# Layer 0's in-degrees from packed tiles: adds on GpSimd and one-column products instead of ones-products of every tile

## The chip, the cores and the metric

One core of a Trainium2 chip runs the kernel alone; seven cores are idle. The metric is device time in microseconds (us) of one execution. The engines are PE (TensorE, matrix products), PEld (its weight loads), DVE (VectorE), ACT (ScalarE), POOL (GpSimd) and SP (here only an issuer of DMAs). Each works through its own list of instructions in order; an instruction that waits for another engine holds up all that stand behind it on its own.

## What is computed

The input is a feature matrix `x` of 2708 x 512 and a 0/1 adjacency matrix `adj` of 2708 x 2708 in int32. Four graph layers follow each other, each on the layer-normed, rectified output of the one before, and each is added to its input. Only layer 0 is touched:

```python
h = relu(layernorm(x))
a = adj.astype(float32)
out = (a.T @ h) @ weight
in_degree = a.sum(axis=0)                    # column sums of adj
out = out * clip(in_degree, 1.0, None)[:, None] ** (-0.5)
x = x + relu(out)
```

Layers 1 to 3 need the transposed 0/1 pattern and the row sums of `adj`, and layer 0's pass over `adj` prepares both.

## The kernel before

The 2708 rows are cut into `NC` = 22 blocks of `R` = 128 rows (the last has 20). The 22 column blocks are cut into six **groups** g of 4, 4, 4, 4, 3 and 3 blocks (line 104). Layer 0 goes through 6 x 22 units (g, m): group g of columns against row block m. A group's results gather in PSUM, one bank of 128 x 512 for each of its `K` column blocks (`acc`, line 577); PSUM has 8 such tiles (`ps`, line 125), which are used in rotation.

`staged` (line 244) writes the program as a software pipeline: in step s it emits `load0` of unit s, `count0` of unit s-4, `sign0` of s-5 and `multiply0` of s-7 (lines 660 to 668). While group 0 runs, the layer norm of `x` and the products with the weight (`h_ps`, line 186) are made too, so PE has twice the work in that group.

- `load0` (487) fetches a 128 x 512 int32 tile `ai` of `adj` (10 buffers). Row blocks 0 to 19 are fetched in pairs, rows 2r of a pair in one tile and rows 2r+1 in the next.
- `count0` (518): ACT squares `ai` into the fp32r tile `ar` (523), which PE will use. DVE makes the running row sum `cum` in int16 (scan, 529) and copies its last column into `deg` (537). For every even m DVE packs two tiles into one int16 tile, `two` = 256 * next + this (541), three buffers. `two` has an int16 for each column, whose low byte is one row's 0 or 1 and whose high byte is the next row's.
- `sign0` (553): ACT turns `cum` into a sum of signs.
- `multiply0` (567): POOL starts the DMA that writes `two` to DRAM (574), from where layer 1 fetches it transposed. PE multiplies `ar` with the halves of `h0[m]` into `acc` (403), two matmuls for each column block, one for m = 21.

The **in-degrees** are column sums of `adj`, so they are sums over partitions, which PE makes: with each of the 22 tiles of a group, K products with a 128 x 32 tile of ones (`oneb`, 592). The tile is read as bf16, every second half-word, which is exact for 0 and 1. They come in batches after m = 3, 7, 11, 15 and 19 (lines 580 to 598; the last takes m = 16 to 21) and add up to 484 matmuls. The sums lie along the free dimension; at m = 19 ACT copies them to SBUF (`by_col`, 601), at m = 21 PE transposes them (607), and DVE, ACT and DVE make `nrm` = max(sum, 1) ** -0.5 of them (611, 618, 619). At the end of the group the K banks of `acc` are scaled by `nrm` and rectified, the even ones on ACT (645), the odd ones on DVE (640), into three buffers of the tag "t", and POOL adds `x` (648; DVE does it in the last group). The next group's fourth `acc` reuses the bank of the first of these.

`fenced` (509) sets a priority: `count0` and `sign0` of later units are put behind the named ACT and DVE instructions of the eviction, so that the tile scheduler doesn't emit them first. The scheduler decides the order on each engine when the program is built; it puts some `two` instructions ahead of scans.

After the last unit `deg` is written to DRAM and fetched back transposed as `rdeg` (685 to 692), and DVE waits for that (695) ahead of the layer norms of layer 1. Layer 1's first products (`nb_ps`, `line_ps`, line 186) begin while layer 0's last group runs.

Of the kernel before, what the change touches and what calls it, by code (L numbers as in the profile page):

```python
# [8 lines left out]
F32 = mybir.dt.float32  # L9
F32R = mybir.dt.float32r  # L10
BF16 = mybir.dt.bfloat16
I32 = mybir.dt.int32
I8 = mybir.dt.int8
I16 = mybir.dt.int16
AF = mybir.ActivationFunctionType
# [29 lines left out]
def fast_layers(  # L45
# [46 lines left out]
    def rows(c):  # L92
        return min(R, N - c * R)
# [358 lines left out]
    with ExitStack() as ring_ctx:  # L452
# [30 lines left out]
        with tc.tile_pool(name="l0", bufs=2) as wk:  # L483
            units = [(g, m) for g in range(len(groups)) for m in range(NC)]
            tiles, uppers, acc, sums, xs = {}, {}, {}, {}, {}
# [32 lines left out]
            def count0(i):  # L518
# [20 lines left out]
                if m % 2 == 0:  # L539
                    two = wk.tile([R, WG + P - R], I16, name="two", bufs=3)  # L540
                    nc.vector.scalar_tensor_tensor(
                        two[:, :wide],
                        tiles[i + 1][0][:, :wide],
                        256.0,
                        ai[:, :wide],
                        op0=ALU.mult,
                        op1=ALU.add,
                    )
                    if wide < KR + P - R:
                        nc.gpsimd.memset(two[:, wide : KR + P - R], 0)  # L550
                tiles[i] = ar, cum, two
# [15 lines left out]
            def multiply0(i):  # L567
# [11 lines left out]
                uppers[m] = ar.bitcast(BF16)  # L579
                batch = range(0)  # L580
                if m == NC - 3:
                    for j in (1, 2):
                        uppers[m + j] = tiles[i + j][0].bitcast(BF16)
                    batch = range(m // 4 * 4, NC)
                elif m % 4 == 3:
                    batch = range(m - 3, m + 1)
                if m == 3:
                    sums[g] = ps.tile([P, 2 * P], F32, name="sums_ps", tag="ps")
                for j in batch:
                    q = rows(j)  # L590
                    for k in range(K):
                        nc.tensor.matmul(
                            sums[g][k * 32 : (k + 1) * 32, :R],
                            oneb[:q],
                            uppers[j][:q, 2 * k * R + 1 : 2 * (k + 1) * R : 2],
                            start=(j == 0),
                            stop=(j == NC - 1),
                        )
                if m == NC - 3:
                    by_col = sums[g, 0] = common.tile([P, D], F32, name="by_col", tag="t", bufs=3)[:, :R]  # L600
                    ins = nc.scalar.copy(by_col[: K * 32], sums[g][: K * 32, :R])
                    fences["act"] = ins.ins
                for k, c in enumerate(cs):
                    matmuls(acc[c], h0[m], ar, k, m)
                if m == NC - 1:
                    pt = sums.pop(g)[:R, P:]
                    nc.tensor.transpose(
                        pt[:, : K * 32], sums.pop((g, 0))[: K * 32], ident[: K * 32, : K * 32]
                    )
                    nrm = sums[g, 1] = small.tile([R, KMAX, 1], F32, name="nrm")  # L610
                    nc.vector.tensor_scalar(
                        nrm[:, :K],
                        pt[:, : K * 32].rearrange("p (k j) -> p k j", j=32)[:, :, :1],
                        1.0,
                        None,
                        op0=ALU.max,
                    )
                    nc.scalar.activation(nrm[:, :K], nrm[:, :K], AF.Sqrt)
                    ins = nc.vector.reciprocal(nrm[:, :K], nrm[:, :K])
                    fences["dve"] = ins.ins  # L620
# [9 lines left out]
                nrm = sums.pop((g, 1))  # L630
# [1401 lines left out]
```

## Time and profile before

| | |
|---|---|
| three runs | 1802.83 us median, 1800.16 to 1804.46 |
| profiled execution | 1800.19 us, its span 1798.3 us |
| granted TensorE clock | 0.995 of full speed |
| PE busy | 1767.9 us (98% of the span) |
| DVE busy | 1309.7 us (73%) |
| ACT busy | 816.0 us (45%) |
| POOL busy | 248.7 us (14%) |
| `sums_ps` products, line 592 | 484 matmuls, 14.2 us busy |
| scans, line 529 | 132, mean 1.18 us with `deg` and 1.21 us without |

The span's first 36 us prepare fused weights for layer 3. Layer 0 takes the stretch from about 39 to 376 us: start and group 0 to 174 us, three groups of four column blocks of 43.2 us each, two groups of three to 376 us. Layer 1 then runs to about 760 us, and layers 2 and 3 take the rest. Busy times are unions of an engine's instructions; matmuls are pipelined, so a busy PE can still be waiting. What ended an idle stretch is inferred from semaphore events.

### The profile page before, as it was taken

The page shows a single profiled execution, that of the slowest core. Times are in us where ns is not written, and L with a number is a line of the kernel's source. Part 1 is how long each engine was busy: PE and PEld are TensorE (multiplying, and loading weights), DVE is VectorE, ACT ScalarE, POOL GpSimd, SP SyncE. Part 2 cuts the span into 40 slices and gives each one's busy share as a digit, 9 for nine tenths or more (in the row PEclk, how much of TensorE's full clock was granted, in tenths as well). Part 3 has the DMA queues.
Part 4 walks back from the last instruction along what each step waited for, and adds up shares of the span by engine and source line. Part 5 has one row for each costly group of instructions (what it writes and reads, how often), then busy time and mean ns, then how long its engine had stood idle before and what let it go on. Part 6 is the DMA issues. An engine that isn't in the chain of part 4 may idle for free.

```text
span 1798.3 us, 30708 instructions
## 1 busy us (share of the span) xinstructions
PE 1767.9 (98%) x11880; PEld 1050.8 (58%) x11880; DVE 1309.7 (73%) x1842; ACT 816.0 (45%) x1554; POOL 248.7 (14%) x245
## 2 busy tenths in 40 slices
PE   9899999999999999999999999999999999999998
PEld 4456777654448888644454444444444455588786
DVE  4952998855446655888999999999999777633334
ACT  2643777732210000156887767767774566400000
POOL 0101332311111211266000000000001222100000
PEclk9999999999999999999999999999999999999999
DMA  7632666634451211243220121121022444313221
GB/s 251 199 106 71 210 204 192 205 80 119 122 142 50 69 55 47 86 147 123 74 62 25 45 63 44 27 63 50 19 68 60 141 134 133 107 43 99 71 71 40
DMA packets 166445, 176.06 MB, mean 98 GB/s; under 512 B 83454, under 2 KB 105918, under 8 KB 165394
## 3 DMA queue, kind: packets, MB, share of 16 engines
q1 hardware_dynamic: 143738, 130.61, 25.7%
q10 hardware_dynamic: 18808, 33.37, 4.9%
q0 software_dynamic: 3744, 10.03, 1.5%
q8 instruction: 95, 1.56, 0.4%
q14 instruction: 60, 0.49, 0.1%
HBM read 110.60 MB, written 55.36 MB: 92 GB/s over the span
## 4 chain that ended last, share of the span: by engine, by line
PE 86%; DVE 7%; issue 3%; DMA 3%; ACT 1%; POOL 1%; DVEq 0%; SPq 0%; ACTq 0%; POOLq 0%
PE acc L403 33%; PE av L1110 19%; PE nb_ps L186 8%; PE sums L1110 6%; PE wh_ps L186 4%; PE self_ps L186 4%; PE line_ps L186 4%; DVE t L923 3%; PE h_ps L186 3%; PE hT_ps L239 2%; PE fused_ps L347 2%; DVE cum L529 2%; DMA ai<-in_adj 1%; DMA degd<-deg 1%; PE av_ps L1063 1%
## 5 line engine op out<-in xcount | busy, mean ns | idle before, releaser
L923 DVE SCALAR_TENSOR_TENSOR t<-rb,ec,vT 128x2708 f32<-128x2708 f32 (+2 forms) x220 | 529.5, 2461 | 13.2 <-PE sums L1110 8.2
L1110 PE MATMUL av<-t,whs 128*32 128x451 f32 (+3 forms) x4576 | 436.7, 515 | 0.9 <-DVE ln_mv L218 0.9
L403 PE MATMUL acc<-halves,kt 128*128 128x512 f32 x1848 | 433.3, 394 | 2.4 <-DVE kt L777 2.1
L403 PEld LDWEIGHTS acc<-halves,kt 128*128 128x128 f32 x1848 | 345.8, 188 | 86.0 <-DVE kt L777 6.6
L1110 PEld LDWEIGHTS av<-t,whs 128*32 128x32 f32 (+1 forms) x4576 | 166.5, 110 | 198.3 <-issue 170.8
L403 PE MATMUL acc<-halves,ar 128*128 128x512 f32 x924 | 233.3, 405 | 3.3 <-ACT ar L523 2.4
L941 ACT ACTIVATE b<-t,eb 128x2708 bf16<-128x2708 f32 (+3 forms) x91 | 218.0, 2396 | 36.2 <-DVE t L923 34.6
L403 PEld LDWEIGHTS acc<-halves,ar 128*128 128x128 f32 x924 | 170.4, 188 | 52.5 <-issue 6.9
L777 DVE SCALAR_TENSOR_TENSOR kt<-lastr,index,vT 128x512 fp32r<-128x512 int16 (+3 forms) x154 | 111.4, 735 | 75.9 <-PE acc L403 75.5
L220 ACT ACTIVATE ln_rs<-ln_mv,eps 128x1 f32<-128x1 f32 x88 | 25.4, 292 | 295.0 <-DVE ln_mv L218 285.6
L1349 DVE CAST kt<-vT 128x512 fp32r<-128x512 uint8 (+3 forms) x154 | 56.4, 368 | 138.2 <-PE acc L403 138.2
L1077 POOL TENSOR_SCALAR z<-y 128x512 f32<-128x512 f32 x22 | 44.1, 2004 | 655.3 <-DVE y L1070 646.4
L1110 PE MATMUL sums<-t,whs 128*32 128x338 f32 (+4 forms) x1464 | 131.7, 449 | 0.8 <-ACT out L1151 0.8
L529 DVE TENSOR_TENSOR_SCAN cum<-ai,deg 128x512 int16<-128x512 int32 (+2 forms) x110 | 128.0, 1176 | 0.5 <-DMA ai<-in_adj 0.5
L911 ACT ACTIVATE whs<-wh,ef 128x64 f32<-128x64 f32 x220 | 76.5, 348 | 99.4 <-PE sums L1110 47.6
L557 ACT ACTIVATE cum<-cum,limit 128x512 int16<-128x512 int16 (+3 forms) x132 | 88.0, 667 | 55.8 <-DVE deg L537 54.9
L1110 PEld LDWEIGHTS sums<-t,whs 128*32 128x32 f32 (+1 forms) x1464 | 54.6, 109 | 62.2 <-issue 32.2
L216 DVE BATCH_NORM_STATS2 ln_st<-x 128x6 f32<-128x512 f32 x88 | 60.2, 684 | 35.6 <-DMA x<-x 22.5
L186 PE MATMUL h_ps<-w0s,hT 128*128 128x512 f32 x168 | 78.5, 611 | 2.3 <-DVE deg L537 1.4
L186 PE MATMUL nb_ps<-wfn,hT 128*128 128x512 f32 x168 | 78.5, 611 | 2.1 <-ACT hT L241 2.1
L241 ACT ACTIVATE hT<-hT_ps 128x512 f32<-128x512 f32 x88 | 51.8, 589 | 54.4 <-PE hT_ps L239 52.8
L523 ACT ACTIVATE ar<-ai 128x512 fp32r<-128x512 int32 (+2 forms) x132 | 74.9, 567 | 2.4 <-DMA ai<-in_adj 2.4
(202 smaller groups left out, 1911.9 us busy)
## 6 DMA issues: line engine op xcount, KB each, us to landing
x<-x SPq DMA_DIRECT2D x105, 256.0 KB
ai<-in_adj SPq DMA_DIRECT2D x84, 256.0 KB
x<-x ACTq DMA_DIRECT2D x84, 256.0 KB
x<-in_x SPq DMA_DIRECT2D x42, 256.0 KB
rb<-rT SPq DMA_DIRECT2D x7, 1354.0 KB
wh<-whd SPq DMA_DIRECT2D x70, 96.0 KB
packed<-two POOLq DMA_DIRECT2D x44, 128.0 KB, 3.7
whd<-wh SPq DMA_DIRECT2D x21, 256.0 KB
```

What stands on the lines that cost most here:

```text
L186: nc.tensor.matmul(po[:n], lhsT[:, f, :n], w[:, f, :], start=(f == 0), stop=(f == NF - 1))
L216: nc.vector.bn_stats(st[:n], xc[:n])
L403: nc.tensor.matmul(acc[:R], weight[:, k * R : (k + 1) * R], parts[:, i, :], start=(m == 0 and i == 0), stop=(m == NC - 1),)
L523: nc.scalar.activation(ar[:, :gw], ai[:, :gw], AF.Square, accum_out=squares[:R, m, g : g + 1])
L529: nc.vector.tensor_tensor_scan(cum[:n, :gw], ai[:n, :gw], ai[:n, :gw], 0.0 if g == 0 else deg[:n, m : m + 1], op0=ALU.add, op1=ALU.max,)
L557: nc.scalar.activation(cum[:n, :gw], cum[:n, :gw], AF.Sign, bias=limit[:n], scale=-1.0, accum_out=signs[:n, m, g : g + 1],)
L777: nc.vector.scalar_tensor_tensor(by_chunk(kt, cs), lastr[:, cs[0] * R : (cs[-1] + 1) * R].rearrange("p (c r) -> p c r", r=R), index[:R, m ...
L911: ins = nc.scalar.activation(t[:q, :O], wh.pop((u, m))[:q], AF.Copy, scale=by)
L923: ins = nc.vector.scalar_tensor_tensor(t[:q, : hi - lo], row[h][:q, lo:hi], ec[:q, m, h : h + 1], vT[g][:q, k, lo:hi], op0=ALU.max, op1=AL ...
L941: nc.scalar.activation(b[:q, : hi - lo], weight[s][:q, : hi - lo], AF.Sigmoid, bias=eb[:q, m, h : h + 1], scale=STEEP,)
L1110: nc.tensor.matmul(p[j * S : (j + 1) * S, : b - a], lhsT, rhs[:, part * size + a : part * size + b], start=(s % NC == 0), stop=(s % NC == ...
L1349: nc.vector.tensor_copy(by_chunk(kt, cs), pattern(m, cs))
```

## The change

The column sums of a group's first 20 row blocks are no longer made by PE from each `ar`. The nine `two` tiles of m = 2 to 18 are added to that of m = 0 on POOL, as int32 numbers with two int16 each, into the new tile `total` (one buffer): 9 adds of 128 x 256 int32 in a group of four, 128 x 192 in a group of three, 54 in all. No byte overflows, as each holds at most 10. At m = 20 DVE adds the low and the high bytes of `total` into the bf16 tile `by_row` (one instruction). After the main matmuls of m = 19 PE takes for each column block three products with one column of `oneb`, and now `by_row` and the tiles of m = 20 and 21 are the weights and the ones are what moves: 12 matmuls of one column in a group of four, 9 in a group of three, 66 in all. The sums then lie along the partitions, so the copy `by_col` and the transpose fall away, and `nrm` is made at m = 19 instead of m = 21. `two` has four buffers instead of three.

In the built program POOL's list now alternates between an add and the DMA of the same `two`; at the end of a group the add of the next group's m = 2 and its DMA stand in front of the four adds of `x`. On DVE `nrm` now stands behind the scan of the next group's m = 0 (before: behind that of its m = 2); the scans of m = 1 and 2 and the packing of m = 2 stand between `nrm` and the two evictions (before: `nrm` and the evictions were neighbours). `by_row` stands one scan behind the last `two` that is added, and waits for POOL.

```diff
@@ -482,7 +482,8 @@
 
         with tc.tile_pool(name="l0", bufs=2) as wk:
             units = [(g, m) for g in range(len(groups)) for m in range(NC)]
-            tiles, uppers, acc, sums, xs = {}, {}, {}, {}, {}
+            tiles, acc, sums, xs = {}, {}, {}, {}
+            pairs, by_rows = {}, {}
 
             def load0(i):
                 g, m = units[i]
@@ -537,7 +538,7 @@
                 nc.vector.tensor_copy(deg[:n, m : m + 1], cum[:n, gw - 1 : gw])
                 two = None
                 if m % 2 == 0:
-                    two = wk.tile([R, WG + P - R], I16, name="two", bufs=3)
+                    two = wk.tile([R, WG + P - R], I16, name="two", bufs=4)
                     nc.vector.scalar_tensor_tensor(
                         two[:, :wide],
                         tiles[i + 1][0][:, :wide],
@@ -548,6 +549,24 @@
                     )
                     if wide < KR + P - R:
                         nc.gpsimd.memset(two[:, wide : KR + P - R], 0)
+                    if m == 0:
+                        pairs[g] = two
+                    elif m < NC - 2:
+                        total = pairs[g]
+                        if m == 2:
+                            total = wk.tile([R, WG], I16, name="total", bufs=1)
+                        nc.gpsimd.tensor_tensor(
+                            total[:, :KR].bitcast(I32),
+                            pairs[g][:, :KR].bitcast(I32),
+                            two[:, :KR].bitcast(I32),
+                            ALU.add,
+                        )
+                        pairs[g] = total
+                    else:
+                        both = pairs.pop(g)[:, :KR].bitcast(mybir.dt.uint8)
+                        both = both.rearrange("p (w e) -> p e w", e=2)
+                        by_row = by_rows[g] = wk.tile([R, WG], BF16, name="by_row", bufs=1)
+                        nc.vector.tensor_tensor(by_row[:, :KR], both[:, 0], both[:, 1], ALU.add)
                 tiles[i] = ar, cum, two
 
             def sign0(i):
@@ -576,46 +595,28 @@
                     for c in cs:
                         acc[c] = ps.tile([P, D], F32, name="acc", tag="ps")
 
-                uppers[m] = ar.bitcast(BF16)
-                batch = range(0)
-                if m == NC - 3:
-                    for j in (1, 2):
-                        uppers[m + j] = tiles[i + j][0].bitcast(BF16)
-                    batch = range(m // 4 * 4, NC)
-                elif m % 4 == 3:
-                    batch = range(m - 3, m + 1)
-                if m == 3:
-                    sums[g] = ps.tile([P, 2 * P], F32, name="sums_ps", tag="ps")
-                for j in batch:
-                    q = rows(j)
-                    for k in range(K):
-                        nc.tensor.matmul(
-                            sums[g][k * 32 : (k + 1) * 32, :R],
-                            oneb[:q],
-                            uppers[j][:q, 2 * k * R + 1 : 2 * (k + 1) * R : 2],
-                            start=(j == 0),
-                            stop=(j == NC - 1),
-                        )
-                if m == NC - 3:
-                    by_col = sums[g, 0] = common.tile([P, D], F32, name="by_col", tag="t", bufs=3)[:, :R]
-                    ins = nc.scalar.copy(by_col[: K * 32], sums[g][: K * 32, :R])
-                    fences["act"] = ins.ins
                 for k, c in enumerate(cs):
                     matmuls(acc[c], h0[m], ar, k, m)
-                if m == NC - 1:
-                    pt = sums.pop(g)[:R, P:]
-                    nc.tensor.transpose(
-                        pt[:, : K * 32], sums.pop((g, 0))[: K * 32], ident[: K * 32, : K * 32]
+                if m == NC - 3:
+                    by_row = by_rows.pop(g)
+                    uppers = [(by_row, 1, R)]
+                    uppers += [(tiles[i + j][0].bitcast(BF16), 2, rows(m + j)) for j in (1, 2)]
+                    pt = ps.tile([P, KMAX], F32, name="sums_ps", tag="ps")
+                    for k in range(K):
+                        for j, (upper, e, q) in enumerate(uppers):
+                            nc.tensor.matmul(
+                                pt[:R, k : k + 1],
+                                upper[:q, e * k * R + e - 1 : e * (k + 1) * R : e],
+                                oneb[:q, :1],
+                                start=(j == 0),
+                                stop=(j == len(uppers) - 1),
+                            )
+                    nrm = sums[g] = small.tile([R, KMAX, 1], F32, name="nrm")
+                    nc.vector.tensor_scalar(
+                        nrm[:, :K, 0], pt[:R, :K], 1.0, None, op0=ALU.max
                     )
-                    nrm = sums[g, 1] = small.tile([R, KMAX, 1], F32, name="nrm")
-                    nc.vector.tensor_scalar(
-                        nrm[:, :K],
-                        pt[:, : K * 32].rearrange("p (k j) -> p k j", j=32)[:, :, :1],
-                        1.0,
-                        None,
-                        op0=ALU.max,
-                    )
-                    nc.scalar.activation(nrm[:, :K], nrm[:, :K], AF.Sqrt)
+                    ins = nc.scalar.activation(nrm[:, :K], nrm[:, :K], AF.Sqrt)
+                    fences["act"] = ins.ins
                     ins = nc.vector.reciprocal(nrm[:, :K], nrm[:, :K])
                     fences["dve"] = ins.ins
                 if g == len(groups) - 1 and m in AHEAD:
@@ -627,7 +628,7 @@
                         xs[c] = load_x(x_in, c, tag=tag, bufs=bufs)
                 if m < NC - 1:
                     return
-                nrm = sums.pop((g, 1))
+                nrm = sums.pop(g)
                 for k, c in enumerate(cs):
                     n = rows(c)
                     xc = xs.pop(c)
```

## The prediction

> **What bounds the kernel now.** I read the busy shares in 40 slices first, then sums by stretch, then what DVE waited for, and last DVE's timeline across one group boundary. In the slices (45 us each) PE is full nearly everywhere, but DVE is at 8 or 9 tenths from the fifth to the eighth slice, the stretch of layer 0's groups 1 to 5, and POOL at 1 to 3:
>
> ```profile
> PE   9899999999999999999999999999999999999998
> ...
> DVE  4952998855446655888999999999999777633334
> ...
> POOL 0101332311111211266000000000001222100000
> ```
>
> The sums by stretch, cut from one `nrm` (line 611) to the next, show PE full in a group of four column blocks, with DVE busy for 39.4 of 43.2 us. In group 4 (three blocks) PE is not full: 34.2 of 37.5 us.
>
> ```profile
> core 0: us, PE busy (x) PEld busy (x) DVE busy (x) ACT busy (x) POOL busy (x), PEclk, DMA share, GB/s
> ...
> 217.19:260.36 43.17, 43.17 (x262) 33.33 (x261) 39.42 (x59) 32.15 (x92) 13.36 (x16) 1.00 0.66 210
> ...
> 303.53:341.03 37.50, 34.16 (x197) 25.05 (x196) 31.84 (x66) 27.07 (x93) 13.32 (x19) 1.00 0.55 172
> ```
>
> The few us that DVE is not busy are no slack. Its waits from 174 to 368 us:
>
> ```profile
> DVE nrm L611 <- PE sums_ps L607: 10.3, 4, 7.5
> DVE two L541 <- DMA packed<-two: 8.3, 8, 1.4
> DVE y L640 <- POOL x L648: 5.8, 4, 1.5
> ```
>
> Only the first is waiting for PE: 7.45 us at the end of group 0, then 0.77, 0.28 and 1.82. So after group 0 DVE reaches each boundary less than 2 us before PE: two engines bound this stage, and whatever DVE is given beyond that moves the end. The timeline of DVE shows the price list:
>
> ```profile
> 260.36 0.16 DVE L611 TENSOR_SCALAR nrm<-sums_ps 128x4 f32<-128x4 f32 x1 [0.28 <-PE sums_ps L607]
> ...
> 263.22 0.75 DVE L640 TENSOR_SCALAR y<-acc,nrm 128x512 f32<-128x512 f32 x1 [1.46 <-POOL x L648]
> 263.88 3.79 DVE L529 TENSOR_TENSOR_SCAN cum<-ai,deg 128x512 int16<-128x512 int32 x2
> ...
> 267.64 1.67 DVE L541 SCALAR_TENSOR_TENSOR two<-ai 128x512 int16<-128x512 int32 x1
> ...
> 269.31 2.44 DVE L529 TENSOR_TENSOR_SCAN cum<-ai,deg 128x512 int16<-128x512 int32 x2
> ...
> 271.72 0.68 DVE L541 SCALAR_TENSOR_TENSOR two<-ai 128x512 int16<-128x512 int32 x1
> ...
> 279.85 0.69 DVE L541 SCALAR_TENSOR_TENSOR two<-ai 128x512 int16<-128x512 int32 x1 [1.24 <-DMA packed<-two]
> ```
>
> The same two scans take 3.79 us while POOL adds `x` (line 648, 261.9 to 268.8 us) and 2.44 us afterwards, the same packing 1.67 and 0.68 us. POOL's add of two SBUF tensors holds DVE up. Of a 512-wide one, 1.28 us alone, DVE loses 0.97 us (a scan of 2.24 for 1.27, a packing of 1.67 for 0.68). An eviction, whose input is in PSUM, does not suffer (0.75 both ways), nor do scans beside POOL's DMA issues and memsets (1.27).
>
> **PE: what goes, what comes.** The chain of work in time order shows a batch of products as 0.35 us, the long one as 0.57:
>
> ```profile
> 289.96 0.35 PE sums_ps L592 x15
> 290.30 7.66 PE acc L403 x32
> 297.96 0.57 PE sums_ps L592 x24
> ```
>
> A group of four loses 4 x 0.35 + 0.57 = 1.97 us of PE; the transpose is nearly covered (0.03 us between matmuls). It gains 12 products of one column, each with a weight load of its own. The trace has none like it. Below: 0.02 us each (16 of the old ones in 0.35 us); above: 0.14 us (the f32 load of the layer norm's transposes; their four take 0.44 us). I take 0.1, the nearest in kind, 1.2 us a group, so PE gains 0.8 us a group, about 5 us in six groups, where PE is the bound.
>
> **POOL and DVE: the adds.** 9 adds a group read two SBUF tensors, the operands of the form that holds DVE up. Nearest row: line 976 in layer 2, f32 128x256, 0.72 us alone. Beside one of these a DVE product of 20x512, 0.67 us at its shortest, takes 1.18:
>
> ```profile
> 843.54 0.73 POOL L976 TENSOR_TENSOR wh_a<-wh_a 128x256 f32<-128x256 f32 x1
> 843.63 1.18 DVE L970 TENSOR_TENSOR wh_a<-wh,arows 20x512 f32<-20x512 f32 x1
> ```
>
> DVE began 0.09 us after POOL and lost 0.51, so it was let go 0.60 us after POOL's start. For 512 elements the same sum gives 1.14 us (at 770 us: 1.74 for 0.69), and a full DVE loses 0.97 of these, 0.17 less. So an add of 256 costs a full DVE 0.43 us, and one of 192, by the slope of 2.1 ns an element, 0.30. Integers may go at another speed; bounds are 0 (memsets cost DVE nothing) and 0.97 us (the 512-wide add). I take 0.43 and 0.30.
>
> The Trainium skill, page SBUF — State Buffer, section "SBUF: two separate sides", says that DVE and GpSimd share one port pair under an exclusive lock, taken for a whole instruction, also by a DVE instruction with two SBUF inputs; this speaks against the change. The trace agrees in kind, but DVE loses 0.97 of 1.28 us and not all. By the rule each add would cost its full 0.72 (0.58 for 192), and the sum below would be some 14 us larger.
>
> **A group of four, DVE's own time:**
> - 9 adds, one of them beside an eviction that doesn't suffer: 8 x 0.43 = +3.4 us.
> - `by_row`: two SBUF inputs of 512, like the packing: +0.68.
> - The wait of `by_row` for POOL: it stands one scan behind the last `two`, the scan will have the memory first, and the add runs behind it: +0.7 (bounds 0 and 1.3, a scan). Behind it wait all later scans, so ACT's signs and tiles.
> - At the boundary the next group's add and DMA issue (0.54) now stand ahead of POOL's adds of `x`, for which the second eviction waits (1.46 now): +0.35 (bounds 0 and 1.3, both in full).
> - Gone: the waits for PE, 0.77 and 0.28: -0.5. The packing's wait for its DMA (1.33, 1.24): a fourth buffer gives 3 us more, but each DMA is issued 1 to 2 us later, behind its add: -0.9 (bounds -1.3 and 0).
>
> Together +3.7 us a group, while PE needs 0.8 less: PE idles, DVE decides.
>
> **The sum.** Start and group 0: from 45 to 85 us DVE is busy for 38 of 40 us and the chain runs through its scans; about six adds fall there, 6 x 0.43 = +2.5 us until PE is full at 90 us. From there to 174 us PE is the bound and DVE idles, so the rest of group 0's adds are hidden (without that cover: 1.3 us), and PE gains 0.8. The `nrm` at m = 19 stops DVE two units earlier, in step with PE's two units, but the evictions now wait behind two scans and a packing (3.07 us by the timeline, against 2.9 us of PE's work): +0.3. Sum +2.0. Groups 1 to 3: 3 x 3.7 = 11.2, less 1.3 since the wait of 1.82 us goes at the last boundary: +9.9. Group 4: adds 9 x 0.30 = 2.7, `by_row` 0.5, its wait 0.6, the queue 0.4, less 2.1 of the 3.6 us that packing waits for DMAs there: +2.1. Group 5: 2.7 + 0.5 + 0.6, less 1.0 of 1.4: +2.8. At the end `deg` leaves when DVE is done (367.6 us), and DVE waits to 381 us for its return; layer 1's products hang on that, so the shift is passed on in full. 2.0 + 9.9 + 2.1 + 2.8 = **+16.8 us**, 1817 us against the profiled execution's 1800.2. The three runs' median is 2.6 us above that execution; I put half of that on top: **1818 us**.
>
> **Rivals.**
> 1. *Faster: DVE has room after all.* It decides if the adds fit into what DVE waits for: 0.5 us at the boundary and 1.3 us for DMAs, less 0.7 for `by_row`, leave 1.1 us for nine adds, 0.12 us each. Then PE's 5 us come home, and the fourth buffer gives up to 5 us in groups 4 and 5: 1790 to 1797. For it: the adds could fall beside casts and evictions. Against it: the row of 843.63.
> 2. *No change.* Small losses (0.2 us an add, no wait for `by_row`) and no more waits for DMAs: 3 x (1.6 + 0.7 - 0.5 - 1.3) and about 0 in groups 4 and 5, +1 at the start: about +2.5 us, 1800 to 1806.
> 3. *Slower still: a wait in place of the one removed.* If an integer add holds DVE like the 512-wide row (0.97), 48 adds on the path (six, 24, 18) cost 0.54 to 0.67 more each, some 28 us; if instead `by_row` and the packing wait longer behind POOL's list, 1 to 2 us a group. 1826 to 1846.
> 4. *That it doesn't do what it says* is excluded: the built program has 54 adds on POOL and 66 products on PE.
>
> **Chances.** Forecast (1806 to 1826) 0.69, rival 3 0.14, rival 2 0.10, rival 1 0.07. The range of 1804 to 1838 reaches into rivals 2 and 3 and leaves the ends of them out. 0.2% is 3.6 us, about what a measurement can tell: faster than 1799.2 0.07, within 0.10, slower 0.83.
>
> **What would show it.** Right: line 529's mean above 1.18 us; DVE's wait for `nrm` at three boundaries gone; PE idle for some us in each of groups 1 to 3, now 46 to 47 us long; POOL's adds with 0.7 us alone and up to 2 us behind a scan; a wait of `by_row` for POOL; all after layer 0 as before, some 17 us later. Wrong: if PE still is full from 174 to 303 us, or if the scans' mean stays, then rival 1 or 2 holds; if the adds take over 1 us alone, rival 3.

## The result, and the profile after

The changed kernel takes **1815.9 us** (median of 4 runs, 1814.6 to 1817.2) against 1803.4 (4 runs, 1800.2 to 1804.5) on the same chip: ratio 1.0073, 95% interval [1.0058, 1.0088], so 0.7% slower. The profiled execution took 1815.0 us, its span 1813.2 against 1798.3. All but about 1 us of the loss arises before 551 us, where layer 1's first aggregation product (a product with the tile `kt`) starts; from there to the end it is 1262.6 us against 1261.5.

The slices of the changed kernel first:

```profile
PE   9999999889999999999999999999999999999998
...
DVE  4942999955545665787989999999999777633334
...
POOL 0301445621110221157000000000000222100000
```

POOL has gone from 2 or 3 tenths to 4 to 6 in the fifth to eighth slice, DVE is at 9 in all four, and PE, which was at 9 before, has the eighth and ninth slices at 8. By stretch (us, PE, PEld, DVE, ACT and POOL busy with instruction counts, granted clock, DMA share, GB/s), from `nrm` to `nrm`:

```profile
171.81:218.16 46.35, 44.24 (x194) 34.61 (x195) 43.16 (x61) 31.97 (x91) 22.79 (x25) 1.00 0.61 188
218.16:264.47 46.31, 42.51 (x180) 33.70 (x179) 43.11 (x61) 31.85 (x91) 22.76 (x25) 0.93 0.64 198
```

A group of four takes 46.3 us where it took 43.2, DVE is busy for 43.1 instead of 39.4, and PE idles for 2 to 4 us. DVE's waits from 172 to 385 us (us in total, times, longest):

```profile
DVE y L641 <- POOL x L649: 8.0, 4, 2.0
DVE by_row L569 <- POOL total L558: 2.5, 5, 0.6
```

After group 0 no wait for PE is left, and none of the packing for its DMA (8.3 us before). In their place stand the evictions' wait for POOL's adds of `x`, 8.0 instead of 5.8, and `by_row`'s for the last add. DVE's timeline across the boundary and the group that begins at 264 us (start, duration):

```profile
264.47 0.15 DVE L615 TENSOR_SCALAR nrm<-sums_ps 128x4 f32<-128x4 f32 x1
...
270.81 0.75 DVE L641 TENSOR_SCALAR y<-acc,nrm 128x512 f32<-128x512 f32 x1 [2.02 <-POOL x L649]
271.48 5.29 DVE L530 TENSOR_TENSOR_SCAN cum<-ai,deg 128x512 int16<-128x512 int32 x2
...
277.40 2.87 DVE L530 TENSOR_TENSOR_SCAN cum<-ai,deg 128x512 int16<-128x512 int32 x2
...
288.54 1.76 DVE L530 TENSOR_TENSOR_SCAN cum<-ai,deg 128x512 int16<-128x512 int32 x1
...
299.38 0.69 DVE L569 TENSOR_TENSOR by_row<-total 128x512 bf16<-128x512 uint8 x1 [0.56 <-POOL total L558]
```

and POOL's in the same stretch:

```profile
268.21 0.74 POOL L558 TENSOR_TENSOR total<-two 128x256 int32<-128x256 int32 x1 [6.95 <-DVE deg L538]
268.90 0.56 POOL L593 DMA_DIRECT2D packed<-two  x1
269.48 5.03 POOL L649 TENSOR_TENSOR x<-x,y 128x512 f32<-128x512 f32 x4
277.56 1.64 POOL L558 TENSOR_TENSOR total<-total,two 128x256 int32<-128x256 int32 x1 [3.06 <-DVE deg L538]
```

An add alone takes 0.74 us; the one of 277.56 stands behind a scan, takes 1.64, and the pair of scans takes 2.87 us where 2.43 is its undisturbed time (264.99 us). From 215 to 345 us the mean of line 530 is 1409 ns (1215 ns for the same stretch of the kernel before):

```profile
L530 DVE TENSOR_TENSOR_SCAN cum<-ai,deg 128x512 int16<-128x512 int32 (+1 forms) x67 | 93.3, 1409 | 0.0
```

What PE idles for is seen at the start of the group of 218 us:

```profile
218.77 9.50 PE L403 MATMUL acc<-halves,ar 128*128 128x512 f32 x40
232.07 30.58 PE L403 MATMUL acc<-halves,ar 128*128 128x512 f32 x120 [3.80 <-ACT ar L524]
```

PE runs through what lies ready (40 matmuls, 0.237 us each), stands still for 3.8 us since DVE and with it ACT are behind, and comes back slower: 120 matmuls at 0.255 us, in a group with a granted clock of 0.93. That costs nothing here, since no `nrm` waits for PE.

### The profile page after: what moved, and what is told of

The parts are those of the page before. It is cut to its first block, busy times and chain, and to the rows that moved or that the text cites. A ratio compares the mean times of both kernels' runs of the same rounds, so it can differ in the third digit from the quotient of the medians.

```text
span 1813.2 us, 29966 instructions
## 1 busy us (share of the span) xinstructions
PE 1765.8 (97%) x11456; PEld 1052.3 (58%) x11456; DVE 1328.1 (73%) x1848; ACT 814.8 (45%) x1548; POOL 302.5 (17%) x299
## 4 chain that ended last, share of the span: by engine, by line
PE 76%; DVE 13%; DMA 5%; issue 3%; POOL 1%; ACT 1%; SPq 0%; DVEq 0%; POOLq 0%; ACTq 0%
PE acc L403 25%; PE av L1111 19%; PE nb_ps L186 8%; PE sums L1111 6%; DVE cum L530 5%; PE self_ps L186 4%; PE line_ps L186 4%; PE wh_ps L186 3%; DVE t L924 3%; PE h_ps L186 2%; PE hT_ps L239 2%; PE fused_ps L347 2%; DMA ai<-in_adj 1%; DVE two L542 1%; DMA packed<-two 1%
## 5 line engine op out<-in xcount | busy, mean ns | idle before, releaser
L1111 PEld LDWEIGHTS av<-t,whs 128*32 128x32 f32 (+1 forms) x4576 | 166.0, 110 | 198.5 <-issue 171.5
L403 PEld LDWEIGHTS acc<-halves,ar 128*128 128x128 f32 x924 | 176.2, 192 | 67.8 <-ACT ar L524 15.4
L530 DVE TENSOR_TENSOR_SCAN cum<-ai,deg 128x512 int16<-128x512 int32 (+2 forms) x110 | 144.2, 1326 | 0.0
L912 ACT ACTIVATE whs<-wh,ef 128x64 f32<-128x64 f32 x220 | 76.6, 348 | 99.4 <-PE sums L1111 46.4
L186 PE MATMUL nb_ps<-wn,hT 128*128 128x512 f32 x168 | 77.8, 607 | 1.2 <-ACT hT L241 1.2
```

The source lines that it names most:

```text
L186: nc.tensor.matmul(po[:n], lhsT[:, f, :n], w[:, f, :], start=(f == 0), stop=(f == NF - 1))
L403: nc.tensor.matmul(acc[:R], weight[:, k * R : (k + 1) * R], parts[:, i, :], start=(m == 0 and i == 0), stop=(m == NC - 1),)
L530: nc.vector.tensor_tensor_scan(cum[:n, :gw], ai[:n, :gw], ai[:n, :gw], 0.0 if g == 0 else deg[:n, m : m + 1], op0=ALU.add, op1=ALU.max,)
L912: ins = nc.scalar.activation(t[:q, :O], wh.pop((u, m))[:q], AF.Copy, scale=by)
L1111: nc.tensor.matmul(p[j * S : (j + 1) * S, : b - a], lhsT, rhs[:, part * size + a : part * size + b], start=(s % NC == 0), stop=(s % NC == ...
```

## The experiments

All medians below stand beside 1802 to 1803.4 us for the kernel before on the same chip; as the chips differ, the ratios to it compare better than the medians. The stages by profile, in us (from `nrm` to `nrm`; the changed kernels make `nrm` two row blocks earlier, so that their second column has two row blocks of four column blocks in the place of two of three, 0.7 us of PE's time, and their third column two row blocks more; both are compared only within a kind):

| | groups 1, 2, 3 | group 4 | from there to the end of `deg` | from there to layer 1's first product with `kt` |
|---|---|---|---|---|
| before | 43.2, 43.2, 43.2 | 37.5 | 26.5 | 169.3 |
| after | 46.4, 46.3, 45.7 | 37.9 | 30.0 | 172.6 |
| before, four buffers | 43.2, 43.2, 43.2 | 35.8 | 25.6 | 170.6 |
| before, buffers and adds | 45.1, 45.1, 43.9 | 36.6 | 27.5 | 171.8 |
| after, three buffers | 46.3, 46.4, 46.0 | 39.4 | 30.2 | 172.7 |
| after, one add | 43.1, 43.1, 43.1 | 36.7 | 28.3 | 172.1 |
| after, memsets | 43.0, 43.1, 43.1 | 36.7 | 28.1 | 173.4 |
| after, copies | 43.3, 44.6, 43.0 | 36.9 | 28.6 | 171.5 |
| after, adds on DVE | 43.5, 43.4, 43.0 | 36.1 | 30.4 | 173.0 |
| after, evictions on ACT | 45.1, 45.0, 44.4 | 36.3 | 30.1 | 173.5 |
| after, late `rdeg` | 46.4, 46.3, 45.8 | 38.4 | 29.9 | 165.4 |
| before, late `rdeg` | 43.2, 43.2, 43.2 | 37.0 | 26.6 | 168.4 |
| after, all moved | 41.4, 41.4, 41.4 | 33.7 | 27.3 | 164.9 |
| before, all moved | 43.2, 43.2, 43.2 | 33.0 | 23.1 | 169.6 |

**The fourth buffer alone** (in the kernel before):

```diff
-                    two = wk.tile([R, WG + P - R], I16, name="two", bufs=3)
+                    two = wk.tile([R, WG + P - R], I16, name="two", bufs=4)
```

> The kernel before with four buffers for `two` and nothing else of the change. Theory (DVE is the bound of groups 1 to 5, and POOL's adds hold it up): DVE's 8.3 us of waits for the packing's DMAs go; groups 1 to 3 stay at 43.2 us, since PE bounds them then, groups 4 and 5 get about 3 and 1 us shorter: 1797 to 1801 us. Rival (the fourth buffer is worth nothing, the waits only move): 1803 us, and DVE waits for the same DMAs or a little later.

1801.1 us, ratio 0.9995 [0.9985, 1.0005]. Groups 1 to 3 don't move: PE is full there. Group 4 gains 1.7 us. Of the packing's 8.3 us of waits for its own DMA 1.1 are left, but 2.4 us of other waits have come (1.9 for the DMA of `ai`). The buffer is not what makes the change slow, nor worth much without it.

**The adds alone**: the kernel before with four buffers and the change's 54 adds on POOL; nobody reads `total`, and the in-degrees are made by PE as before.

```diff
+                    if m == 0:
+                        pairs[g] = two
+                    elif m < NC - 2:
+                        total = pairs[g]
+                        if m == 2:
+                            total = wk.tile([R, WG], I16, name="total", bufs=1)
+                        nc.gpsimd.tensor_tensor(total[:, :KR].bitcast(I32),
+                            pairs[g][:, :KR].bitcast(I32), two[:, :KR].bitcast(I32), ALU.add)
+                        pairs[g] = total
```

> The kernel before with four buffers and the 54 adds on GpSimd, whose sum nothing reads; PE still makes the in-degrees. Theory: each add takes 0.43 us from DVE in groups 1 to 3 and 0.30 in groups 4 and 5, so groups 1 to 3 take about 45 us instead of 43.2, and the run is 8 to 12 us slower than with four buffers alone: 1807 to 1811 us. Rival (the loss is from the new waits, of `by_row` and of the evictions behind POOL's list, and the adds are hidden): within 3 us of four buffers alone.

1809.7 us, 1.0035 [1.0023, 1.0048]; 8.6 us more than with the buffer alone. Adds whose result nothing waits for cost most of what the change costs. They first eat what DVE had spare in a group: its waits for PE go, the group becomes 1.9 us longer, and PE idles.

**The change with three buffers:**

> The changed kernel with three buffers for `two`. Theory: the packing waits for its DMA again, which is now issued behind an add: 1 to 2 us a group in five groups, 1821 to 1825 us. Rival (the buffer was worth nothing): 1816 us and no such waits.

1822.1 us, 1.0107 [1.009, 1.0123]. The number is as expected, the reason is not. The profiled execution, the fastest of the four, is 3.4 us above the change's; 1.9 of these arose before the first product of layer 0, and 1.5 in group 4. Groups 1 to 3 stay nearly the same. The packing waits four times in groups 3 to 5, 4.0 us together, for the add that still reads its buffer. In the full groups the buffer is worth next to nothing: a gain there was expected in vain.

**One add instead of nine**: only that of m = 2 is left; the in-degrees miss the row blocks 4 to 19, `by_row` and the 12 products stay.

```diff
                         if m == 2:
                             total = wk.tile([R, WG], I16, name="total", bufs=1)
-                        nc.gpsimd.tensor_tensor(
+                            nc.gpsimd.tensor_tensor(
```

> The changed kernel with one of the nine adds of a group; the in-degrees then miss 16 of 20 row blocks. `by_row`, its wait, the products and the early `nrm` stay. Theory: groups 1 to 3 fall from 46.3 to 42.5 to 43 us, groups 4 and 5 by 2 us each, the start by 2: about 1798 to 1802 us. Rival (waits and queue order make the loss): 1810 to 1814 us.

1800.0 us, 0.9988 [0.9978, 0.9998]. Groups 1 to 3 fall to 43.1 us. So eight adds carry the loss of these groups: 3.3, 3.2 and 2.6 us, 0.33 to 0.41 each. That includes `by_row`'s wait, and it is a net figure, since DVE of this kernel still waits 0.4 to 1.0 us for PE at the end of each of these groups. The scans' mean from 215 to 345 us in this kernel, against the 1409 ns above:

```profile
L530 DVE TENSOR_TENSOR_SCAN cum<-ai,deg 128x512 int16<-128x512 int32 (+2 forms) x71 | 89.6, 1279 | 0.0
```

**Eight memsets of 128x640 int32 in the place of the eight adds**, 0.66 us each (the in-degrees miss the same row blocks):

```diff
+                        else:
+                            blank = wk.tile([R, 640], I32, name="blank", bufs=1)
+                            nc.gpsimd.memset(blank, 0)
```

> The changed kernel with one real add a group and a memset of 128x640 int32 on GpSimd in place of each of the eight others (in-degrees miss row blocks). A memset keeps POOL busy for about as long but reads no SBUF. Theory (two engines reading SBUF get in each other's way): like one add alone, groups 1 to 3 of about 43.1 us, 1800 us. Rival (POOL's occupied list, its DMA issues and the evictions' adds behind it make the loss): like the change, 46.3 us and 1815 us.

1802.7 us, 1.0000 [0.999, 1.001]. The run answers less than it was meant to: a memset depends on nothing, so all 48 were placed ahead, between 45 and 95 us, and none ran in groups 1 to 5. In that stretch, though, the two engines can be compared, since POOL was busy for 36.5 of 45 us, 28.6 of them with these memsets, and DVE for 42.8. From 45 to 90 us, with the memsets:

```profile
L530 DVE TENSOR_TENSOR_SCAN cum<-ai 128x512 int16<-128x512 int32 x19 | 22.5, 1205 | 0.2 <-DMA ai<-in_adj 0.2
L542 DVE SCALAR_TENSOR_TENSOR two<-ai 128x512 int16<-128x512 int32 x9 | 6.1, 674 | 0.0
L230 DVE TENSOR_SCALAR hn<-x,ln_mv,ln_rs 128x512 f32<-128x512 f32 x7 | 5.7, 818 | 0.0
```

and in the kernel with one add and no memsets:

```profile
L530 DVE TENSOR_TENSOR_SCAN cum<-ai 128x512 int16<-128x512 int32 x20 | 23.8, 1206 | 0.3 <-DMA ai<-in_adj 0.3
L542 DVE SCALAR_TENSOR_TENSOR two<-ai 128x512 int16<-128x512 int32 x10 | 6.8, 677 | 0.0
L230 DVE TENSOR_SCALAR hn<-x,ln_mv,ln_rs 128x512 f32<-128x512 f32 x7 | 3.7, 530 | 0.0
```

Memsets on POOL, which only write SBUF, take nothing from the scans and the packings. They are not free for all of DVE: the layer norm's seven `hn` take 2.0 us more, and in the profiles group 0 of this kernel ends 2.5 us later than with one add. For the scans and packings of groups 1 to 5 a busy POOL is thus not enough to explain the cost; whether its long list is, the next run asks.

**Eight copies of `two` in the place of the eight adds** (one SBUF input instead of two; the in-degrees miss the same row blocks):

```diff
+                        else:
+                            copied = wk.tile([R, WG], I16, name="copied", bufs=1)
+                            nc.gpsimd.tensor_copy(
+                                copied[:, :KR].bitcast(I32), two[:, :KR].bitcast(I32))
```

> The changed kernel with one real add a group and a copy of 128x256 int32 on GpSimd in place of each of the eight others: one input from SBUF instead of two (in-degrees miss row blocks). If every POOL instruction that reads SBUF stops DVE for most of its time, the loss goes with the copy's length: some 0.2 to 0.3 us each, groups 1 to 3 of 44.7 to 45.5 us, 1807 to 1812 us. If only the second input collides: like one add alone, 43.1 us and 1800 us.

1804.4 us, 1.0007 [0.9997, 1.0017], between the two expectations. Two groups are as with one add, and one is 1.5 us longer, where the packing waited for a buffer that a copy still read; in the profile another 1.9 us arose before the end of group 0 and was not followed up. POOL's list has as many entries here as in the changed kernel, and the groups are short all the same. A copy on POOL in group 2,

```profile
227.81 1.31 POOL L566 COPY copied<-two 128x256 int32<-128x256 int32 x1 [3.05 <-DVE deg L538]
```

and the two scans beside it:

```profile
227.66 2.54 DVE L530 TENSOR_TENSOR_SCAN cum<-ai,deg 128x512 int16<-128x512 int32 x2
```

The copy, 0.40 us at its shortest, waits for a scan to end and takes 1.31; the scans take 0.11 us more than 2.43, less than expected. So it is not enough that POOL reads SBUF. Whether the add costs more for its second input or for its length (0.74 us) was not told apart.

The Trainium skill, page SBUF — State Buffer, section "SBUF: two separate sides", gives an exclusive lock for a whole instruction between a DVE instruction with two SBUF inputs and a GpSimd one that reads SBUF. The runs agree that scans and packings lose nothing to memsets (1205 and 1206 ns) and that the second comer waits (copy 1.31, add 1.64 us behind a scan). They disagree on the size: DVE lost 0.44 to 0.49 us to an add that takes 0.74, and 0.11 to a copy of 0.40.

**The adds on DVE**, as int16:

```diff
-                        nc.gpsimd.tensor_tensor(
-                            total[:, :KR].bitcast(I32), pairs[g][:, :KR].bitcast(I32),
-                            two[:, :KR].bitcast(I32), ALU.add)
+                        nc.vector.tensor_tensor(
+                            total[:, :KR], pairs[g][:, :KR], two[:, :KR], ALU.add)
```

> The changed kernel with its adds on DVE, as int16 and 512 wide. Against the change it saves 9 x 0.41 us of collisions, by_row's wait (0.56) and part of the eviction's wait, and pays nine adds: at the packing's 0.68 us groups 1 to 3 take 47 to 48 us and the run 1818 to 1822; if 16-bit data goes twice as fast, 0.35 us, they take 44 to 45 us and the run 1806 to 1811. By the theory, DVE's sum decides, on whichever engine the adds stand.

1806.6 us, 1.002 [1.0008, 1.0032], 9 us better than the change. DVE's own adds from 215 to 345 us:

```profile
L558 DVE TENSOR_TENSOR total<-total,two 128x512 int16<-128x512 int16 (+1 forms) x24 | 9.0, 375 | 0.0
```

The mean is of two widths, 0.40 us for 128x512 and 0.34 for 128x384. DVE does for 0.40 us what costs it up to 0.49 us when POOL does it. It also saves `by_row`'s wait, and the evictions wait 1.3 instead of 2.0 us, as no add stands ahead of POOL's adds of `x`. Moving this work off DVE was worth less than nothing to DVE.

**All evictions of groups 0 to 4 on ACT**, in the changed kernel:

```diff
-                    if k % 2:
+                    if k % 2 and g == len(groups) - 1:
```

> The changed kernel with all of a group's evictions on ACT, except in the last group. DVE loses two evictions of 0.75 us and the wait of 2.0 us for POOL. Theory (DVE's sum decides): groups 1 to 3 fall from 46.3 to 42.5 to 43 us, near what PE needs (about 42.2), 1804 to 1807 us. Rival (ACT now waits for POOL's adds of x and holds up the signs and tiles behind it): 45 to 47 us, 1812 to 1818 us.

1808.5 us, 1.0035 [1.0021, 1.0049], between the two expectations. DVE is rid of two evictions and 2 us of waiting a group, 3.5 us, and the group falls by only 1.3. Where the rest went is seen in line 542, the packing, from 215 to 345 us (654 ns in the changed kernel):

```profile
L542 DVE SCALAR_TENSOR_TENSOR two<-ai 128x512 int16<-128x512 int32 (+2 forms) x34 | 34.8, 1028 | 0.2
```

POOL's adds of `x`, which had run while DVE waited for them, now run beside DVE's scans and packings. DVE's wait had been the cover of these adds. A wait was turned into collisions.

**The hand-over to layer 1: `rdeg` late.** At the end of layer 0 `deg` is sent to DRAM and returns as `rdeg`; on DVE the operation that waits for it, line 696, stands ahead of group 5's `nrm`. DVE of the changed kernel:

```profile
393.03 0.18 DVE L696 TENSOR_SCALAR rcnt<-rdeg 128x22 f32<-128x22 f32 x1 [13.71 <-DMA rdeg<-degd]
...
394.16 0.15 DVE L615 TENSOR_SCALAR nrm<-sums_ps 128x3 f32<-128x3 f32 x1
```

ACT, whose square root of `nrm` stands ahead of the copy that PE needs:

```profile
394.35 0.20 ACT L618 ACTIVATE nrm<-nrm 128x3 f32<-128x3 f32 x1 [14.03 <-DVE nrm L615]
394.86 1.21 ACT L646 ACTIVATE acc<-acc,nrm 128x512 f32<-128x512 f32 x2 [0.30 <-DVE nrm L620]
396.01 0.57 ACT L241 ACTIVATE hT<-hT_ps 128x512 f32<-128x512 f32 x1
```

and PE, which has ended group 5 at 383.84 us, has work for one row block of layer 1, and then stands still:

```profile
387.71 3.60 PE L186 MATMUL line_ps<-wl,hT 128*128 128x512 f32 x8
394.30 1.11 PE L239 MATMUL hT_ps<-ident,hn 128*128 128x128 f32 x4 [2.99 <-DVE hn L230]
396.63 5.87 PE L186 MATMUL nb_ps<-wn,hT 128*128 128x512 f32 x8 [1.22 <-ACT hT L241]
```

In the kernel before, the same operation on DVE ended its wait at 381.22 us, and PE, which had work for two row blocks, stood still for only 1.3 us up to 402 us:

```profile
381.22 0.18 DVE L695 TENSOR_SCALAR rcnt<-rdeg 128x22 f32<-128x22 f32 x1 [12.40 <-DMA rdeg<-degd]
...
392.38 0.66 PE L239 MATMUL hT_ps<-ident,hn 128*128 128x128 f32 x4 [1.28 <-DVE hn L230]
```

In the changed kernel eight products take 5.87 us instead of 3.60 after the two gaps, and from 396 to 402 us the granted clock is 0.58:

```profile
396.00:402.00 6.00, 5.37 (x8) 2.31 (x9) 2.50 (x5) 1.67 (x4) 0.00 (x0) 0.58 0.52 185
```

The Trainium skill, page TensorE: Matmul & The Clock Gate, section "Why this matters for your kernels", asks for no idle gaps beyond some 3 us. This stretch fits it: a clock of 0.58 behind gaps of 3.0 and 1.2 us, and 1.00 from 396 to 402 us in the kernel before, whose gap was 1.3. But 3 us is no border in these runs: behind a gap of 1.89 us the kernel with copies had a clock of 0.50 from 228.8 to 232.2 us, and behind one of 3.38 us the changed kernel with three buffers kept 1.00 from 280.1 to 287 us.

The edit moves the four operations behind group 5's evictions:

```diff
-        nc.vector.tensor_scalar(rcnt, rdeg, float(NEIGHBORS), 1.0, op0=ALU.min, op1=ALU.max)
+        with tc.issue_after(fences["dve"]):
+            nc.vector.tensor_scalar(rcnt, rdeg, float(NEIGHBORS), 1.0, op0=ALU.min, op1=ALU.max)
...
```

> The change with one order altered: on DVE the four operations on rdeg and rcnt (lines 696 to 699), which wait for the return of deg from DRAM, stand behind group 5's nrm, evictions and adds of x and no longer ahead of them. In the changed kernel DVE's rcnt waits 13.7 us until 393.0, nrm waits behind it, ACT's Sqrt waits for nrm, and ACT's copy hT behind that Sqrt; TensorE stands still for 3.6 and 1.6 us and then runs at a granted clock of 0.58 from 396 to 402. Theory A: this queue is where the shift grows between the end of the in-degrees (+10.5 us) and layer 1's first aggregation product (+13.8). Then the copy runs at once, TensorE has work until the round trip ends, the stage from the end of the in-degrees to that product falls from 172.6 to 167 to 169 us, and the median is 1810 to 1813 us beside 1816 for the changed kernel. Rival B: the stage is set by what comes later (casts and tiles of layer 1 that hang on rdeg itself); then the stage stays at 172 to 173 us and the median at 1815 to 1817.

1810.2 us, 1.0036 [1.0023, 1.0049] against 1.0073 [1.0058, 1.0088]. On DVE the two lines have changed places,

```profile
383.08 0.16 DVE L615 TENSOR_SCALAR nrm<-sums_ps 128x3 f32<-128x3 f32 x1 [1.48 <-PE sums_ps L607]
...
394.73 0.18 DVE L697 TENSOR_SCALAR rcnt<-rdeg 128x22 f32<-128x22 f32 x1 [7.05 <-DMA rdeg<-degd]
```

and PE goes on without a gap:

```profile
389.05 3.60 PE L186 MATMUL line_ps<-wl,hT 128*128 128x512 f32 x8
392.48 0.60 PE L239 MATMUL hT_ps<-ident,hn 128*128 128x128 f32 x4
392.92 3.60 PE L186 MATMUL nb_ps<-wn,hT 128*128 128x512 f32 x8
```

The stage falls by 7.2 us, beyond what was expected. Its profiled execution reaches `kt` 5.9 us earlier than the changed kernel's and ends only 2.6 earlier; where it lost the 3.3 us between was not followed up, and the median shows the most of the gain.

**The same in the kernel before:**

> The same order on DVE in the kernel before: rcnt and rdeg behind group 5's nrm and evictions. There TensorE stands still for only 1.5 us at the end of the round trip, since it finished group 5 8.3 us after the in-degrees (5.8 in the changed kernel). Theory A (the two queues stand behind DVE's wait, and the change uncovers that) expects 0 to -1.5 us: 1801 to 1803.5. Rival B (the order of these four operations is worth the same few us to any kernel, and has nothing to do with the change) expects -3 to -6 us: 1797 to 1800.

1800.8 us, 0.9991 [0.9982, 1.0]; the stage falls by 0.9 us. The order was nearly free before the change: PE had ended group 5 8.3 us after `deg`, not 5.8, and so had work for most of the round trip. The change took that cover away. The round trip itself, from the end of `deg` to `rcnt`, is not the same in each run either: 13.7 us in the profile before, 15.0 in that of the changed kernel, 13.7 to 15.4 over all.

**All that the traces point to**: the adds as int16 on DVE, all evictions of groups 0 to 4 on ACT, the adds of `x` on DVE, `rdeg` late.

```diff
-                    eng = nc.gpsimd if g < len(groups) - 1 else nc.vector
+                    eng = nc.vector
```

> The change with all that its traces point to: the nine adds of a group on DVE as int16 (0.395 us each), the evictions of groups 0 to 4 all on ACT, the adds of x on DVE (so that POOL reads no two tensors in layer 0), and rcnt behind group 5's evictions. Theory: DVE's load per group of four is then 0.75 x 2 us less for the evictions, about 1.3 less waiting for POOL, 2.6 more for the four adds of x, and no collisions: about 41 us, under PE's 42.3, so that PE sets groups 1 to 3 at 42.3 to 42.6 us each; the median is 1794 to 1799. Rival: DVE still decides, since it now stands in wait for ACT's evictions before it adds x; groups 1 to 3 at 43.5 us or more, and the median at 1801 to 1807.

**1788.4 us, 0.9922 [0.9908, 0.9935]**: faster than both kernels, and than the 1794 to 1799 expected. The control has the same three moves and the fourth buffer, but the old in-degrees:

> The kernel before with the same three rearrangements and the fourth buffer (evictions of groups 0 to 4 on ACT, adds of x on DVE, rcnt behind group 5's evictions) but the in-degrees by batches of products as they were. PE was full in groups 1 to 3 there, so these should stay at 43.1 to 43.3 us each, and the gains are those of groups 4 and 5 and of the hand-over: 1798 to 1802. Beside the kernel with int16 adds on DVE and the same rearrangements this gives what the shorter products are worth when DVE has room: if that one is 3 to 5 us faster, TensorE's saving of 0.9 us a group comes home; if they are equal, DVE's adds eat it.

1794.3 us, 0.9956 [0.9942, 0.9969], also less than expected. A group of four in the first (PE and DVE busy are the first and third sums),

```profile
212.96:254.30 41.34, 41.34 (x185) 32.94 (x185) 40.75 (x71) 33.13 (x93) 6.47 (x12) 1.00 0.71 222
```

and in the control:

```profile
218.47:261.64 43.17, 43.17 (x262) 33.34 (x261) 38.19 (x61) 33.20 (x94) 6.47 (x12) 1.00 0.68 213
```

PE is full in both, and the shorter products are worth 1.8 us a group, 5.5 us in groups 1 to 3 and 5.8 between the medians. DVE takes 2.6 us more, and now has room for it. Why 1.8, when PE's batches had been counted at less, shows in PE's timeline of the control:

```profile
223.95 0.42 PE L592 MATMUL sums_ps<-ar,oneb 128*32 128x128 bf16 x16
224.30 7.73 PE L403 MATMUL acc<-halves,ar 128*128 128x512 f32 x32
231.96 0.42 PE L592 MATMUL sums_ps<-ar,oneb 128*32 128x128 bf16 x16
```

and of the other:

```profile
218.31 35.11 PE L403 MATMUL acc<-halves,ar 128*128 128x512 f32 x149
253.27 0.18 PE L604 MATMUL sums_ps<-oneb,by_row 128*128 128x1 bf16 x1
```

From start to start, 149 matmuls in a row take 34.96 us, 0.235 each; 32 between two batches take 7.66, 0.239 each, so 0.15 us of a batch's price stand in the matmuls behind it. The five batches' own 1.97 us and five times this, less the 0.95 us of the 12 new products (253.27 to 254.22 us), make 1.8.

The other half is the moves that both kernels share, among them the adds of `x` on DVE. Line 646 from 215 to 345 us in the faster kernel:

```profile
L646 DVE TENSOR_TENSOR x<-x,y 128x512 f32<-128x512 f32 x15 | 9.3, 682 | 0.0
```

DVE adds in 0.68 us; POOL's add, 1.28 us alone, cost DVE 0.97. The control's gain, 7.7 us over the kernel before, is that of groups 4 and 5, 4.5 and 3.5 us. How the gain divides between this move, the evictions and the fourth buffer (1.7 and 0.9 us in these groups by itself) was not measured.

## Why the prediction was right, and where it was wrong

The verdict, the mechanism and the time hold: 1818 us forecast, 1815.9 measured; between the medians the change costs 12.5 us where 15.2 were forecast. That the time fits so well is in part luck, for the steps of the sum miss by more than their sum does: up to the end of `deg` the shift came out 6 us smaller than forecast, behind it 4.4 us larger. The table goes by one profiled execution of each kernel, and that of the kernel before was the fastest of its four. Measured at one mark of DVE's list that both kernels share, the end of a group's last scan (20 rows), the shift grows so:

| step | predicted | measured |
|---|---|---|
| start, groups 0 and 1 | 2.0 + 3.7 | +4.6 (0.9 + 3.7) |
| group 2 | +3.7 | +2.6 |
| group 3 | +3.7 | +3.6 |
| group 4, with the 1.3 less at its first boundary | +0.8 | -1.9 |
| group 5, to the end of `deg` | +2.8 | +1.6 |
| `deg` to layer 1's first product with `kt` | 0 | +3.3 |
| from there to the end | 0 | +1.1 |
| sum, in profiled executions | +16.8 | +14.9 |

- **An add of 256 costs 0.43 us**: right in size, and shown by the runs with and without the adds. Next to a full DVE it lost 0.44 (a pair of scans, 2.87 for 2.43) to 0.49 (1.76 for 1.27), at times less, 0.33 to 0.41 in the mean. The f32 row of layer 2 was the right neighbour: 0.74 and 0.73 us alone. The rival with 0.97 an add is out, and so is the one that finds room on DVE.
- **The group of four, +3.7**: 2.6 and 3.6 in groups 2 and 3. `by_row` takes 0.69 us (forecast 0.68), its wait 0.56 (0.7), the evictions wait 0.56 more (0.35), and the waits for PE are gone, as forecast.
- **The mis-sized term is "gone: the packing's wait for its DMA"**. The step let 0.9 of 1.3 us go in a full group, 2.1 of 3.6 in group 4 and 1.0 of 1.4 in group 5; all 8.3 us went. The fourth buffer alone leaves 1.1 us of it and brings 2.4 us of others; with the adds these are gone too. A packing that comes later because of the adds finds its data and its buffer ready, so part of the adds fell into a wait that was there anyhow. In group 4, from mark to mark, the scans take 2.9 us more, `by_row` and its wait 1.0, other waits 0.7; the waits for DMA (3.6) and PE (1.8) are gone, and the packings take 0.9 less, since they no longer run beside the adds of `x`. Together -1.7. With three buffers part of the packing's wait comes back, now for POOL (4.0 us).
- **Start and group 0**: this was +2.0 in the sum and came out at +0.9: PE's first product of group 0's last row block starts at 173.67 us instead of 172.79, and DVE waits for PE at this boundary in both kernels. The 3.7 us from there to the mark in group 1 are those forecast for that group.
- **The step that failed is "the shift is passed on in full"**: 0 was put for this stage, and it grew by 3.3 us. 1.3 of them are a longer round trip, for which no run gives a reason. The round trip was seen, but not what stands behind DVE's wait for it: group 5's `nrm`, then ACT's square root, then ACT's copy for PE. Before, PE's lag behind DVE hid this queue. As the change brings PE's end nearer to DVE's (5.8 us instead of 8.3) and the round trip is longer, PE runs dry, for 3.0 and 1.2 us, and comes back at a clock of 0.58. Late `rdeg` takes 7.2 us off the stage in the changed kernel and 0.9 in the kernel before: shown.
- **PE's saving, 0.8 us a group, was too small**: 1.8, as the last two runs show, and the faster kernel's groups of 41.4 us lie under the 42.3 expected of it. The 12 products take 0.95 us instead of 1.2, and a batch costs about 0.15 us more than its own time. In the changed kernel it made no difference, since DVE decides. For the rival "faster" it doubles the prize: by an estimate of 1 us a group, a prediction for a kernel in which DVE has room would have been wrong by some 5 us.
- **What would show it**: the scans' mean above 1.18 us (1.33), `nrm`'s wait gone at three boundaries, PE idle in each group, groups near 46 us and adds of 1.64 us behind a scan came true. That everything behind layer 0 comes some 17 us later did not: 10.5 us at the end of `deg`, and 13.8 at layer 1's first product with `kt`.

## What to carry to other kernels

Work moved from a full engine to an idle one isn't free if both read SBUF: here DVE paid about as much for POOL's adds (0.33 to 0.49 us) as for making them itself (0.40 us), and more for POOL's adds of `x` (0.97 against 0.68), so try such work on the full engine first. A saving on PE shows only when the engine that sets the pace has room for what is added; make the room, and the same idea turns from a loss of 0.7% into a gain of 0.3% over the same kernel without it (1788.4 against 1794.3 us; the moves that make the room give the other 0.4%). And before a shift is taken as passed on in full, read what stands in line behind the wait at the hand-over, on each engine, and what covered it so far.

## What the runs showed of the hardware

- POOL's adds in a row kept a scan of DVE waiting: one that started at 271.48 us, with POOL's four adds of `x` running from 269.48 to 274.5, ended at 275.6 and so took 4.1 us, and its pair 5.29 instead of 2.43.
- Both sides lose, and not by the same measure: a copy of 128x256 int32 on POOL went from 0.40 to 1.31 us and cost the two scans beside it 0.11; an add of the same shape went from 0.74 to 1.64 and cost 0.44. Memsets, 28.6 us of POOL's time in 45, cost the scans nothing (1205 and 1206 ns), but the seven `hn`, f32 instructions with one 128x512 input, 2.0 us (818 and 530 ns).
- Behind gaps of 3.0 and 1.2 us PE had a granted clock of 0.58 for 6 us: eight products in 5.87 us instead of 3.60. Gap and clock don't go strictly together: 0.50 for 3.4 us behind a gap of 1.89 us, 1.00 behind one of 3.38.
- 149 matmuls of 128x512 in a row take 0.235 us each, 32 between two batches of sums 0.239.
- An int16 add of 128x512 on DVE takes 0.39 to 0.43 us, a packing of the same width with int32 inputs 0.68.
